# A two-layer convolution with weights made on the chip: loads ordered by marks, and a start-up rearranged

## The chip, the cores and the metric

One core of a Trainium2 chip runs the whole program. Its engines are TensorE (PE, with its weight loads PEld), VectorE (DVE), ScalarE (ACT), GpSimd (POOL) and SyncE (SP), which here issues DMA transfers and computes nothing. The metric is the time of one execution in microseconds.

## The reference

Two layers of the same form, each x = x + conv(groupnorm(x)), on x of shape (32, 32, 64, 256): 32 samples s, 32 positions b, 64 channels, length 256. The convolution has three taps, and its weights differ for every b and every l; they are made by a small network from z:

```python
h = jax.nn.relu(_ln(z @ W1 + b1, g1, be1))              # (32, 256, 128)
w = (h @ W2 + b2).reshape(B, L, CI, CO, K)              # 12288 weights for each (b, l)
hb = jax.nn.relu(_ln(z @ Wb1 + bb1, gb1, beb1))
bias = (hb @ Wb2 + bb2).transpose(0, 2, 1)
x_uf = jnp.stack([xp[..., i:i + L] for i in range(K)], axis=-1)
out = jnp.einsum('sbilk,bliok->sbol', x_uf, w) + bias[None]
```

`groupnorm` cuts the last axis into 32 groups of 8 and takes the mean and variance over all positions, channels and the 8 of the group, separately for each sample.

## The kernel before

**Units and steps.** A unit u is four positions (NT) by a quarter of the length (64 values, LT); a layer has UL = 32 units, the program U = 64. Each unit is worked in two halves of the output channels, so that there are 128 steps v = 2u + h. The main loop (L821) runs v from 1 to 127. In step v TensorE makes the weights of v in twelve groups (`weights`, L739) and, behind the first group's `make`, the convolution of step v - 1 (`products`, L665). `order` (L737) lists the groups: for each of four sets of eight channels the kinds 0, 2, 1. `make` (L615) fills a PSUM tile `pg` (three buffers); `take` (L626) evicts it with b2 added into the tile `wall`: VectorE takes kinds 0 and 1 and half of kind 2 (L634), ScalarE the other half of kind 2 in eight instructions (L645). `products` runs 288 matmuls in four bursts, each into one of two PSUM buffers `pc`, and VectorE adds each burst to the residual in `ring` (L685) and in layer 0 takes statistics of the result for the next layer's norm (`last_stats`, L341).

**Order by hand.** The whole program is emitted in a fixed order, and each engine executes its part in that order. `agenda(v)` (L781) lists what is emitted behind each of the twelve groups. Behind group 0 stands `after(v - 1)` (L725), all on SyncE: the store of the finished half, the load of four pieces of x for the statistics of the first norm (`load_pieces`, until step 42), the residual and the bias of step v + 1 (`load_residual`, `load_bias` with four transfers) and every fourth step the hidden layer (`load_hidden`). Behind group 2 stands `next_half` (L694): GpSimd normalizes half a unit from `raw` or `land` into `xn` (two instructions, L608), and SyncE loads the half after it: one transfer in layer 0, four in layer 1, whose rows are 128 bytes long (L177). Behind group 5 GpSimd adds the bias (`add_bias`, L566). The edges of a half are collected by ScalarE behind group 1 (`take_edges`, L581) and in every second step of layer 0 transposed by TensorE behind group 3 (`turn_edges`, L586), for the neighbours in layer 1.

**Start-up.** `first_phase` (L440) streams x in 22 units of four pieces through three slots of `ring` and one in `land`, while the small network runs in eight batches (`Batch`): ScalarE writes the hidden layer (L302) and the bias (L327), and issues their stores `hd` (L311) and `bd` (L333) itself. The first 18 units (`needed`) give the statistics that the first norm needs. Then come `Merge`, the tables `tab`, `starting` (L759: VectorE normalizes unit 0 in eight pieces, two halves by four cuts), the statistics of the last units, and step 1. The twelve groups of step 0 run inside this phase (`first_weights`).

Of the kernel before, what the change touches and what calls it, by code (L numbers as in the profile page):

```python
# [30 lines left out]
P = 128  # L31
# [12 lines left out]
def conv_layers(  # L44
# [39 lines left out]
    xe = [dram.tile([P, P], FP, name=f"xe_{u}") for u in range(UL)]  # L84
    hd = [dram.tile([P, 2 * BLK], FP, name=f"hd_{i}") for i in range(U // 4)]
    bd = [dram.tile([NT, 2, C, LT], FP, name=f"bd_{i}") for i in range(U // 2)]

# [75 lines left out]
    def load_half(u, k, buf=None):  # L163

        buf = raw if buf is None else buf
        n, q, bg = place_of(u)
        if n == 0:
            nc.sync.dma_start(out=by_slot(buf), in_=xp[u][:, k * NT // 2 : (k + 1) * NT // 2])
            return
        if k == 0:  # L170
            load_edges(u)
        for a in range(2):
            for h in range(NH):
                rows = slice((1 - a) * C + h * CH, (1 - a) * C + (h + 1) * CH)
                src = x1[u - UL][h][k * NT // 2 * S : (k + 1) * NT // 2 * S]
                src = src.rearrange("(t s) (o a m) -> a o t s m", s=S, a=2, m=MT)[a]
                nc.sync.dma_start(out=by_sample(buf)[rows, :, :, a : a + MT], in_=src)  # L177

# [43 lines left out]
    class Batch:  # L222
# [69 lines left out]
        def hidden(self, net):  # L292
            vec = self.w.vec
            ps = []
            for k in range(2):
                p = ps_g.tile([P, 2, BLK], FP, tag="pg", name="ph")
                ps.append(p)
                for r in range(2):
                    x = slice((2 * k + r) * R, (2 * k + r) * R + A + 1)
                    nc.tensor.matmul(p[:, r], self.w.wc[x, net], self.zq[x, net], start=True, stop=True)  # L300
            for k in range(2):
                nc.scalar.activation(  # L302
                    self.ht[net][k],
                    ps[k].rearrange("p r f -> p (r f)"),
                    AF.Relu,
                    bias=vec[:, 2 * net + 1 : 2 * net + 2],
                    scale=vec[:, 2 * net : 2 * net + 1],
                )
                if net:
                    continue  # L310
                nc.scalar.dma_start(out=hd[self.j * NR // 2 + k], in_=self.ht[0][k])  # L311

        def bias(self, i):
            n = 2 * M
            p = ps_c.tile([P, n], FP, tag="pc", name="pb")
            for b in range(2):
# [15 lines left out]
            )  # L332
            nc.scalar.dma_start(  # L333
                out=bd[i].rearrange("t b o l -> (b o) t l"), in_=bs.rearrange("p t a m -> p t (a m)")
# [105 lines left out]
    def first_phase(first_weights, first_bias, add_bias, starting):  # L440
# [22 lines left out]
        with tc.tile_pool(name="stage", bufs=1) as stage:  # L463
# [35 lines left out]

            for i in range(units):  # L500
                j, odd = divmod(i, 2)
# [32 lines left out]
                if i == 6:  # L534
                    for x in range(2):
                        load_hidden(x)
                if i == needed - 2:
                    load_half(0, 1, land)
                    load_residual(0)
                if i == needed - 1:  # L540
                    load_half(0, 0)
                    load_w2(0, CH, C)
                if i == needed:
                    first_bias()
                if i == needed + 1:
                    table.lay(table.spread(), [nc.vector.tensor_copy, nc.scalar.copy])
                    starting()
                first_weights(i - (needed - 11))
            load_residual(1)

    with tc.manual_schedule():
# [73 lines left out]

        def take(pg, n, kind, o0):  # L626

# [36 lines left out]

        def products(v):  # L665
            u, h = divmod(v, NH)
# [3 lines left out]
            for q in range(NB):  # L670
# [23 lines left out]
        def next_half(u, k):  # L694
# [29 lines left out]

        def after(v):  # L725

            u, h = divmod(v, NH)
            store(v)
            load_pieces(v + 1)
            if v + 2 < NH * U:  # L730
                load_residual(v + 2)
                load_bias(v + 2)
            if h == 1 and u % 2 == 1 and u + 3 < U:
                load_hidden((u + 3) // 2)

        starts = range(0, CH, OG)
        order = [(kind, o) for o in starts for kind in (0, 2, 1)]  # L737

        def weights(v, k, between=None):  # L739
# [5 lines left out]
            if between:  # L745
                between()
            take(pg, n, kind, o0)
            if kind == 1 and u % UL == UL - 1 and n + 1 < NL:
# [10 lines left out]
        def starting():  # L759
# [3 lines left out]
            cuts = [0] + [1 + e * (q + 1) for q in range(NB)]  # L763
            for j0, j1 in zip(cuts, cuts[1:]):
                for k in range(2):
                    normalize(0, k, bufs[k], nc.vector, j0, j1)
            load_half(1, 0)

        def first_bias():
            x = xn.rearrange("p n t j s -> p (n t j s)")  # L770
            h = x.shape[1] // 2
            load_bias(0, x[:, h : h + CH * LT].rearrange("p (o l) -> p o l", l=LT))

        first_phase(first_weights, first_bias, add_bias, starting)
# [52 lines left out]
        products(NH * U - 1)  # L827
        after(NH * U - 1)


# [92 lines left out]
```

## Time and profile before

| | us |
|---|---|
| three runs | 4000.01, 4010.09, 4016.39 |
| median | 4010.09 |
| the profiled execution, its own time | 4010.21 |
| its span (first to last instruction) | 4008.4 |
| TensorE busy in the span | 3810.9 |
| VectorE, GpSimd, ScalarE busy | 2592.2, 1939.5, 1285.8 |

The profile is one execution. A row of instructions gives start, duration, engine, line, operation, what it writes and reads, and in brackets the idle time of the engine before it and what ended it. "issue" as the one that ended it means that the engine waited for nothing that the profile shows. SPq and ACTq rows are the issue of transfers, not the transfers.

### The profile page before, as it was taken

Reading aid. Unit: us, or ns where it says so; the run is one execution under the profiler, and the core shown is the slowest. Engines: PE = TensorE matmul, PEld = TensorE weight load, DVE = VectorE, ACT = ScalarE, POOL = GpSimd, SP = SyncE. Lnnn points to the kernel's source line nnn. Section 1 sums busy time; section 2 is a strip of 40 time slices with the busy share of each in tenths; the row PEclk is TensorE's granted clock in tenths of the full one; section 3 lists DMA queues with packets and bytes.
Section 4 is the critical chain, followed back from the end, with each engine's and each line's share of the span. In section 5 each row is a group of like instructions: output and inputs, shape, how many; then the busy total and the mean of one; then the engine's idle time right before and its main releaser. Section 6 shows DMA issues by size and latency. Waiting matters only on the chain.

```text
span 4008.4 us, 185362 instructions
## 1 busy us (share of the span) xinstructions
PE 3810.9 (95%) x86548; PEld 3675.3 (92%) x86548; DVE 2592.2 (65%) x2954; ACT 1285.8 (32%) x4431; POOL 1939.5 (48%) x655
## 2 busy tenths in 40 slices
PE   6699999999999999999999999999999999999999
PEld 3499999999999999999989999999999999999998
DVE  4677777777777776666665555555555555555655
ACT  3423333323333333333323323323233233333332
POOL 2154445444544445544545545555546545645551
PEclk7799999999999999999999999999999999999999
DMA  8666556556556555445488878878788788788782
GB/s 271 233 201 195 180 177 193 177 172 195 177 178 196 173 168 159 134 153 156 134 196 154 148 132 160 145 147 151 140 166 141 140 156 141 147 150 140 157 146 87
DMA packets 644660, 657.76 MB, mean 164 GB/s; under 512 B 562600, under 2 KB 570160, under 8 KB 578096
## 3 DMA queue, kind: packets, MB, share of 16 engines
q1 hardware_dynamic: 624688, 633.30, 65.5%
q8 instruction: 677, 11.09, 1.2%
q10 hardware_dynamic: 19200, 12.59, 1.0%
q14 instruction: 95, 0.78, 0.1%
HBM read 496.91 MB, written 148.90 MB: 161 GB/s over the span
## 4 chain that ended last, share of the span: by engine, by line
PE 80%; DVE 6%; ACT 6%; issue 2%; DMA 1%; POOL 0%; SPq 0%; ACTq 0%; POOLq 0%; DVEq 0%
PE pg L622 49%; PE pc L676 24%; PE pg L623 6%; ACT wall L645 5%; DVE wall L634 4%; DMA bt<-bd 1%; DVE ring L685 1%; DVE parts L341 0%; POOL ring L566 0%; DVE xn L608 0%; PE pe L586 0%; DVE first_parts L723 0%; ACT rim L581 0%; PE over L371 0%; SPq L559 0%
## 5 line engine op out<-in xcount | busy, mean ns | idle before, releaser
L622 PE MATMUL pg<-hT,w2t 128*64 128x128 f32 x24576 | 2752.5, 274 | 26.7 <-issue 24.0
L623 PE MATMUL pg<-hT,w2t 128*64 128x128 f32 x24576 | 2753.3, 274 | 17.0 <-issue 16.7
L622 PEld LDWEIGHTS pg<-hT,w2t 128*64 128x64 f32 x24576 | 2689.0, 137 | 63.9 <-issue 37.9
L623 PEld LDWEIGHTS pg<-hT,w2t 128*64 128x64 f32 x24576 | 2689.2, 137 | 23.1 <-issue 22.7
L634 DVE TENSOR_TENSOR wall<-pg,b 128x1024 f32<-128x1024 f32 (+1 forms) x1536 | 1874.1, 1220 | 726.0 <-PE pg L623 720.1
L645 ACT ACTIVATE wall<-pg,b 64x128 f32<-64x128 f32 x4096 | 1158.8, 465 | 2596.1 <-DVE wall L634 2596.0
L566 POOL TENSOR_TENSOR ring<-ring,bt 128x2048 f32<-128x2048 f32 x127 | 578.1, 4552 | 1200.9 <-DMA bt<-bd 755.1
L676 PEld LDWEIGHTS pc<-wall,xn 128*32 128x32 f32 x36864 | 914.8, 110 | 110.3 <-issue 61.2
L676 PE MATMUL pc<-wall,xn 128*32 128x128 f32 (+1 forms) x36864 | 951.6, 262 | 64.1 <-issue 34.7
L685 DVE TENSOR_TENSOR ring<-pc,ring 128x512 f32<-128x512 f32 x512 | 353.9, 691 | 622.2 <-PE pc L676 617.9
L608 POOL TENSOR_TENSOR xn<-raw,tab 128x2112 f32<-128x2112 f32 x86 | 440.1, 5118 | 447.2 <-PE pc L676 433.7
L608 POOL TENSOR_TENSOR xn<-xn,tab 128x2112 f32<-128x2112 f32 x126 | 591.4, 4693 | 9.9
L608 POOL TENSOR_TENSOR xn<-land,tab 128x2112 f32<-128x2112 f32 x40 | 224.3, 5609 | 111.9 <-DMA land<-x 102.0
L341 DVE BATCH_NORM_STATS2 parts<-ring 128x6 f32<-128x256 f32 x512 | 192.1, 417 | 6.5
L723 DVE BATCH_NORM_STATS2 first_parts<-land 128x6 f32<-128x512 f32 x168 | 114.5, 681 | 0.6 <-DMA land<-in_xg_dram 0.6
L433 POOL COPY tab<-spot 64x1024 f32<-64x1024 f32 x28 | 29.0, 1035 | 94.1 <-ACT spot L420 93.2
L276 POOL TENSOR_TENSOR raw<-w2t,xn 128x256 f32<-128x256 f32 x16 | 10.3, 644 | 113.7 <-DVE xn L271 113.7
L300 PE MATMUL ph<-xn,wc 17*128 17x512 f32 x128 | 34.7, 771 | 26.7 <-DVE xn L266 15.3
L458 DVE BATCH_NORM_STATS2 first_parts<-ring 128x6 f32<-128x512 f32 x72 | 44.2, 676 | 17.3 <-DMA ring<-in_xg_dram 17.3
L300 PEld LDWEIGHTS ph<-xn,wc 17*128 17x128 f32 x128 | 10.0, 214 | 44.2 <-DVE xn L266 19.5
L302 ACT ACTIVATE xn<-ph,vec 128x1024 f32<-128x1024 f32 x32 | 37.5, 1198 | 9.8 <-ACT xn L302 5.7
L586 PEld LDWEIGHTS pe<-ident,rim 128*128 128x128 f32 x32 | 4.5, 139 | 36.0 <-ACT rim L581 36.0
(87 smaller groups left out, 368.8 us busy)
## 6 DMA issues: line engine op xcount, KB each, us to landing
bt<-bd SPq DMA_DIRECT2D x508, 256.0 KB, 10.6
ring<-in_xs_dram SPq DMA_DIRECT2D x64, 1024.0 KB, 11.1
x<-ring SPq DMA_DIRECT2D x64, 1024.0 KB, 4.9
ring<-x SPq DMA_DIRECT2D x64, 1024.0 KB, 9.5
out_dram<-ring SPq DMA_DIRECT2D x64, 1024.0 KB, 4.8
raw<-in_xp_dram SPq DMA_DIRECT2D x55, 1056.0 KB, 14.6
land<-in_xg_dram SPq DMA_DIRECT2D x46, 1024.0 KB, 8.2
raw<-x SPq DMA_DIRECT2D x128, 256.0 KB, 7.7
```

The lines of the kernel that those rows point to most:

```text
L300: nc.tensor.matmul(p[:, r], self.w.wc[x, net], self.zq[x, net], start=True, stop=True)
L341: nc.vector.bn_stats(out, y.rearrange("p o (a m) -> p o a m", a=2)[:, :, :, g * e : (g + 1) * e])
L458: nc.vector.bn_stats(first_parts[:, g, bg], slots[order[i]][:, k])
L566: nc.gpsimd.tensor_tensor(y, y, bts.pop(v), ALU.add)
L608: eng.tensor_tensor(o, i, tab[:, x, None, j0:j1].to_broadcast(list(o.shape)), op)
L622: nc.tensor.matmul(pg[0:C, k, :], w[:, k0 * C : (k0 + 1) * C], h0, start=True, stop=True)
L623: nc.tensor.matmul(pg[C:P, k, :], w[:, k1 * C : (k1 + 1) * C], h1, start=True, stop=True)
L634: nc.vector.tensor_tensor(place(rows, a), pg[rows].rearrange("p o (t m) -> p t m o", t=NT), b2[n][rows, kind, None, None, o0 : o0 + OG].to ...
L645: nc.scalar.activation(place(rows, a)[:, :, :, k], pg[rows, k].rearrange("p (t m) -> p t m", t=NT), AF.Identity, bias=b2[n][rows, kind, o0 ...
L676: nc.tensor.matmul(pc[t * S : (t + 1) * S, n0 - q * EB : n1 - q * EB, :], xn[:, u % 2, t, p, :], wall[:, t, a : a + (n1 - n0) * CH], start ...
L685: nc.vector.tensor_tensor(part, pc.rearrange("p (m a) o -> p o a m", a=2), part, ALU.add)
L723: nc.vector.bn_stats(first_parts[:, g, bg], lands[i % LAND])
```

## The change

Four things are changed together.

1. *Marks.* A mark is a transfer on SyncE of 16 bytes of `wall`, written by the eviction of a named group, to a scratch tensor. SyncE works in order, so what stands behind the mark is issued after that eviction. In step v the residual of v + 1 stands behind the mark of group 2, the half behind group 5 in layer 0, bias and hidden layer behind group 6; in layer 1 the four parts of a half stand behind groups 1, 4, 7 and 9. `after` is gone; store and pieces stay behind group 0. `add_bias` moves from group 5 to 9.
2. *Stores of the small network.* `hd` and `bd` are issued by SyncE.
3. *Start-up.* The bias and the residual of step 0 are loaded earlier, the bias into a free part of `w2`, and added at unit 15 instead of 19. The phase ends two units earlier; the statistics of the last two units, and the normalization of unit 1, go to step 1. `starting` normalizes two of the four cuts at once and the other two behind the first two additions of `products(0)`. In step 0 VectorE alone evicts kind 2. The slots of the last six units change.
4. *Order.* The last set of a step has its kinds in the order 2, 0, 1, and `turn_edges` stands behind group 7 instead of 3.

```diff
-        n, q, bg = place_of(u)
-        if n == 0:
-            nc.sync.dma_start(out=by_slot(buf), in_=xp[u][:, k * NT // 2 : (k + 1) * NT // 2])
-            return
-        if k == 0:
-            load_edges(u)
-        for a in range(2):
-            for h in range(NH):
...
+        nc.sync.dma_start(out=by_slot(buf), in_=xp[u][:, k * NT // 2 : (k + 1) * NT // 2])
+
+    def parts_of_half(u, k, buf):
+
+        def part(a, h):
...
+        return [lambda a=a, h=h: part(a, h) for a in range(2) for h in range(NH)]
...
-                nc.scalar.dma_start(out=hd[self.j * NR // 2 + k], in_=self.ht[0][k])
+                nc.sync.dma_start(out=hd[self.j * NR // 2 + k], in_=self.ht[0][k])
...
-            nc.scalar.dma_start(
+            nc.sync.dma_start(
                 out=bd[i].rearrange("t b o l -> (b o) t l"), in_=bs.rearrange("p t a m -> p t (a m)")
...
-        order = [i % 4 for i in range(needed - 2)] + [0, 1, 2, 1, 2, 1]
+        order = [i % 4 for i in range(needed - 2)] + [1, 2, 1, 2, 1, 2]
...
-            for i in range(units):
+            for i in range(needed + 2):
...
-                    add_bias(0)
...
+                if i == needed // 2:
+                    first_bias(half_w2[:, 0 : CH * LT])
+                if i == needed - 6:
+                    load_residual(0)
+                if i == needed - 3:
+                    add_bias(0)
                 if i == needed - 2:
                     load_half(0, 1, land)
-                    load_residual(0)
...
-                if i == needed:
-                    first_bias()
                 if i == needed + 1:
                     table.lay(table.spread(), [nc.vector.tensor_copy, nc.scalar.copy])
-                    starting()
+                    starting(0)
+                    starting(1)
                 first_weights(i - (needed - 11))
-            load_residual(1)
+        rest = [lambda i=i, k=k: stats(i, range(k, k + 2)) for i in range(needed + 2, units) for k in (0, 2)]
+        return rest
...
-                add_scalar(slice(C, P), CH)
+                (add if alone else add_scalar)(slice(C, P), CH)
...
                 nc.vector.tensor_tensor(part, pc.rearrange("p (m a) o -> p o a m", a=2), part, ALU.add)
+                if between:
+                    between(q)
...
-            u, k = (u, 1) if k == 0 else (u + 1, 0)
-            if u < U:
-                load_half(u, k, place_half(u, k))
+            u, k = half_after(u, k)
+            if UL <= u < U and k == 0:
+                load_edges(u)
...
+        def mark(v, k):
+
+            kind, o = order[k]
+            a = (3 * CH, 0, 2 * CH)[kind] + o
+            nc.sync.dma_start(out=marks[v : v + 1, k], in_=wall[0:1, 0, a : a + 4])
...
-        order = [(kind, o) for o in starts for kind in (0, 2, 1)]
+        order = [(kind, o) for o in starts for kind in ((2, 0, 1) if o == starts[-1] else (0, 2, 1))]
...
+            def cut(q):
+                if q < NB:
+                    for k in range(2):
+                        normalize(0, k, bufs[k], nc.vector, cuts[q], cuts[q + 1])
...
-        normalize(1, 0)
-        load_half(1, 1)
-        add_bias(1)
+
+        def second():
+            load_half(1, 0)
+            normalize(1, 0)
+            load_half(1, 1)
+
+        def cut_next(q):
+            cut(q + 2)
...
-            todo[0].append(lambda: after(v - 1))
-            todo[2].append(lambda: next_half(*((u + 1, 1) if h == 0 else (u + 2, 0))))
+            if v == 1:
+                todo[0].append(second)
+            todo[0].append(lambda: store(v - 1))
+            todo[0].append(lambda: load_pieces(v))
+            half = (u + 1, 1) if h == 0 else (u + 2, 0)
+            todo[2].append(lambda: next_half(*half))
+            x, k = half_after(*half)
+            loads = {}
             if v + 1 < NH * U:
-                todo[5].append(lambda: add_bias(v + 1))
+                loads[4 if v == 1 else 2] = [lambda: load_residual(v + 1)]
+                loads[6] = [lambda: load_bias(v + 1), lambda: hidden_after(v - 1)]
+                todo[9].append(lambda: add_bias(v + 1))
+            if x < UL:
+                loads[5] = [lambda: load_half(x, k, place_half(x, k))]
+            elif x < U:
+                for i, part in zip((1, 4, 7, 9), parts_of_half(x, k, place_half(x, k))):
+                    loads.setdefault(i, []).append(part)
+            if v == 1:
+                for i, f in enumerate(rest):
+                    todo[1 + i].append(f)
+                todo[2].append(lambda: load_residual(1))
+                todo[2].append(lambda: add_bias(1))
+            for i, fs in loads.items():
+                todo[i].append(lambda i=i: mark(v, i))
+                todo[i] += fs
...
                 if h == 1:
-                    todo[3].append(lambda: turn_edges(u))
+                    todo[7].append(lambda: turn_edges(u))
...
-                weights(v, k, (lambda: products(v - 1)) if k == 0 else None)
+                weights(v, k, (lambda: products(v - 1, cut_next if v == 1 else None)) if k == 0 else None)
```

## Rows read from the trace of the kernel before

**Rows 1.** The page: busy time of each engine, its share of the span, instructions.
```profile
PE 3810.9 (95%) x86548; PEld 3675.3 (92%) x86548; DVE 2592.2 (65%) x2954; ACT 1285.8 (32%) x4431; POOL 1939.5 (48%) x655
```

**Rows 2.** Windows: stretch, us, busy PE, PEld, DVE, ACT, POOL, clock, DMA, GB/s.
```profile
0.00:200.00 200.00, 127.50 (x968) 84.01 (x968) 107.52 (x199) 81.94 (x146) 31.99 (x49) 0.75 0.76 252
```

**Rows 3.** Chain of waits: start, us, what; bursts of `products` in layer 0.
```profile
228.40 6.32 PE pc L676 x249
...
468.82 7.28 PE pc L676 x288
499.11 7.14 PE pc L676 x288
527.55 7.28 PE pc L676 x288
```

**Rows 4.** Waits of TensorE: line and releaser: us in total, times, longest us.
```profile
PE pc L676 <- issue: 34.7, 87, 3.1
PE pe L586 <- ACT rim L581: 28.3, 32, 1.0
PE pg L622 <- issue: 24.0, 27, 2.3
PE pg L623 <- issue: 16.7, 21, 2.3
...
PE pc L676 <- ACT wall L645: 12.1, 61, 1.9
```

**Rows 5.** Timeline, end of a step in layer 1: ScalarE, VectorE, TensorE.
```profile
3520.34 2.25 ACT L645 ACTIVATE wall<-pg,b 64x128 f32<-64x128 f32 x8 [2.97 <-DVE wall L634]
...
3520.77 1.22 DVE L634 TENSOR_TENSOR wall<-pg,b 128x1024 f32<-128x1024 f32 x1 [0.53 <-PE pg L623]
...
3522.64 0.63 PE L676 MATMUL pc<-wall,xn 128*32 128x64 f32 x17 [0.17 <-ACT wall L645]
```

**Rows 6.** Timeline of ScalarE and VectorE: after and at stores that ScalarE issues.
```profile
86.22 0.47 ACT L327 ACTIVATE xn<-pb,vec 128x256 f32<-128x256 f32 x1 [0.44 <-PE ph L300]
...
167.20 4.38 ACTq L333 DMA_DIRECT2D bd<-xn  x1
...
168.51 0.15 DVE L384 TENSOR_TENSOR apart<-over,moments 128x9 f32<-128x9 f32 x1
```

**Rows 7.** Timeline of VectorE and GpSimd: `starting` and the first additions.
```profile
178.91 0.76 DVE L608 TENSOR_TENSOR xn<-raw,tab 128x576 f32<-128x576 f32 x1
...
181.05 4.76 DVE L608 TENSOR_TENSOR xn<-land,tab 128x576 f32<-128x576 f32 x1
...
194.69 4.84 DVE L458 BATCH_NORM_STATS2 first_parts<-ring 128x6 f32<-128x512 f32 x8
...
207.23 0.69 DVE L685 TENSOR_TENSOR ring<-pc,ring 128x512 f32<-128x512 f32 x1 [1.87 <-PE pc L676]
...
180.18 5.01 POOL L566 TENSOR_TENSOR ring<-ring,xn 128x2048 f32<-128x2048 f32 x1 [40.78 <-ACT tab L435]
```

**Rows 8.** The page: a DMA queue: packets, MB, share of 16 engines.
```profile
q8 instruction: 677, 11.09, 1.2%
```

**Rows 9.** TensorE after two long issue waits; the window at the second's burst.
```profile
3549.85 0.32 PE L622 MATMUL pg<-hT,w2t 128*64 128x128 f32 x1 [2.30 <-issue]
...
2368.86 0.87 PE L676 MATMUL pc<-wall,xn 128*32 128x128 f32 x12 [3.09 <-issue]
...
2363.00:2366.00 3.00, 2.72 (x102) 2.48 (x102) 0.69 (x1) 0.00 (x0) 0.27 (x1) 1.00 1.63 95
```

**Rows 10.** Windows: products at the change of layers; a step of layer 1.
```profile
2090.00:2101.60 11.60, 7.32 (x282) 6.98 (x283) 4.33 (x9) 0.05 (x1) 0.00 (x0) 1.00 0.88 227
...
3494.20:3501.40 7.20, 7.20 (x290) 7.11 (x292) 2.07 (x3) 0.00 (x0) 7.12 (x3) 1.00 0.02 5
3516.00:3522.00 6.00, 6.00 (x116) 6.00 (x113) 4.42 (x4) 3.03 (x13) 4.79 (x2) 1.00 1.02 110
3502.00:3516.00 14.00, 14.00 (x262) 14.00 (x260) 10.27 (x10) 5.45 (x20) 6.03 (x3) 1.00 1.00 245
```

More of the change, by code (lines that the diff above doesn't have):

```diff
@@ L85, in conv_layers @@
     hd = [dram.tile([P, 2 * BLK], FP, name=f"hd_{i}") for i in range(U // 4)]
+    marks = dram.tile([U * NH, 16, 4], FP, name="marks")
     bd = [dram.tile([NT, 2, C, LT], FP, name=f"bd_{i}") for i in range(U // 2)]
@@ L165, in load_half @@
         buf = raw if buf is None else buf
-        n, q, bg = place_of(u)
-        if n == 0:
-            nc.sync.dma_start(out=by_slot(buf), in_=xp[u][:, k * NT // 2 : (k + 1) * NT // 2])
-            return
-        if k == 0:
-            load_edges(u)
-        for a in range(2):
-            for h in range(NH):
[L174 to L177, printed above, removed]
+        nc.sync.dma_start(out=by_slot(buf), in_=xp[u][:, k * NT // 2 : (k + 1) * NT // 2])
+    def parts_of_half(u, k, buf):
+        def part(a, h):
+            rows = slice((1 - a) * C + h * CH, (1 - a) * C + (h + 1) * CH)
+            src = x1[u - UL][h][k * NT // 2 * S : (k + 1) * NT // 2 * S]
+            src = src.rearrange("(t s) (o a m) -> a o t s m", s=S, a=2, m=MT)[a]
+            nc.sync.dma_start(out=by_sample(buf)[rows, :, :, a : a + MT], in_=src)
+        return [lambda a=a, h=h: part(a, h) for a in range(2) for h in range(NH)]
     def residual(v):
@@ L542, in first_phase @@
                     load_w2(0, CH, C)
-                if i == needed:
-                    first_bias()
                 if i == needed + 1:
                     table.lay(table.spread(), [nc.vector.tensor_copy, nc.scalar.copy])
-                    starting()
+                    starting(0)
+                    starting(1)
                 first_weights(i - (needed - 11))
-            load_residual(1)
+        rest = [lambda i=i, k=k: stats(i, range(k, k + 2)) for i in range(needed + 2, units) for k in (0, 2)]
+        assert len(rest) == 2 * (RING - 1)
+        return rest
     with tc.manual_schedule():
@@ L624, in make, with take @@
             return pg
-        def take(pg, n, kind, o0):
+        def take(pg, n, kind, o0, alone=False):
             def place(rows, a):
@@ L663, in last_stats, with products @@
                     bn_stats(parts[:, g, bg, h, :], residual(v), g)
-        def products(v):
+        def products(v, between=None):
             u, h = divmod(v, NH)
@@ L701, in next_half, with half_after @@
             normalize(u, k, place_half(u, k))
-            u, k = (u, 1) if k == 0 else (u + 1, 0)
-            if u < U:
-                load_half(u, k, place_half(u, k))
+            u, k = half_after(u, k)
+            if UL <= u < U and k == 0:
+                load_edges(u)
+        def half_after(u, k):
+            return (u, 1) if k == 0 else (u + 1, 0)
         pieces = [(j, bg, g) for j in range(1, NQ) for g in range(FIRST[j]) for bg in range(BG)]
@@ L723, in piece, with hidden_after @@
             nc.vector.bn_stats(first_parts[:, g, bg], lands[i % LAND])
-        def after(v):
-            u, h = divmod(v, NH)
[L728 to L732, printed above, removed]
+        def mark(v, k):
+            kind, o = order[k]
+            a = (3 * CH, 0, 2 * CH)[kind] + o
+            nc.sync.dma_start(out=marks[v : v + 1, k], in_=wall[0:1, 0, a : a + 4])
+        def hidden_after(v):
+            u, h = divmod(v, NH)
             if h == 1 and u % 2 == 1 and u + 3 < U:
@@ L746, in weights @@
                 between()
-            take(pg, n, kind, o0)
+            take(pg, n, kind, o0, v == 0)
             if kind == 1 and u % UL == UL - 1 and n + 1 < NL:
@@ L763, in starting, with first_bias @@
             cuts = [0] + [1 + e * (q + 1) for q in range(NB)]
[L764 to L774, printed above, removed]
+            def cut(q):
+                if q < NB:
+                    for k in range(2):
+                        normalize(0, k, bufs[k], nc.vector, cuts[q], cuts[q + 1])
+            return cut
+        def first_bias(buf):
+            load_bias(0, buf.rearrange("p (o l) -> p o l", l=LT))
+        cut = starting()
+        rest = first_phase(first_weights, first_bias, add_bias, cut)
         bp = ctx.enter_context(tc.tile_pool(name="bias", bufs=1))
         load_bias(1)
-        normalize(1, 0)
-        load_half(1, 1)
-        add_bias(1)
+        def second():
[4 more added lines that the diff above has]
+            cut(q + 2)
         def agenda(v):
@@ L827, in conv_layers @@
         products(NH * U - 1)
-        after(NH * U - 1)
+        store(NH * U - 1)
 def _parameters(inputs, n):
```

## The prediction

> **What bounds the kernel now.** The page comes first: TensorE is busy for 95% of the span, every other engine for at most 65% [rows 1]. So a microsecond counts where TensorE idles, and there are two regions. The table by windows shows the first: in the first 200 us TensorE is busy for 127.5, at a mean granted clock of 0.75 [rows 2]. After that the kernel is 127 like steps v, each with one `products` burst and twelve `make` groups; in the chain of waits a burst starts 28.44 us after the one before (499.11 to 527.55) where nothing interferes, and 30.29 us (468.82 to 499.11) where the step has the transposes of `turn_edges` [rows 3]. The waits by engine say what TensorE idles for [rows 4]: "issue", which means that no semaphore of the program ended the wait, 75.4 us in three rows; the transposes at L586 waiting for ScalarE's rim copy, 28.3 us; `products` waiting for ScalarE's last eviction, 12.1 us. The rest of that list is start-up.
>
> **The change part by part.** Durations are those of the profiled execution: 4010.2 us, of which 4008.4 are span. The median of the runs shown, 4010.09, is the same.
>
> *A. `turn_edges` from group 3 to group 7.* The rim copy stands behind ScalarE's eviction of group 1 and is ready 0.9 us after TensorE asks (28.3 by 32 [rows 4]). Four groups later, some 7 us, it has long been done. The transposes themselves stay. 32 waits go: -28 us. Bounds: nothing (if they are late there as well) and -28.3. What is late next in these steps is the next group's weights, which are there. The store of the edges starts 7 us later; it is read a layer later.
>
> *B. Last three groups in the order 2, 0, 1.* Kind 2 has two evictions, VectorE and then ScalarE. Now it is the group before the last: ScalarE's starts at 3520.34 and takes 2.25, so it ends 0.05 before `products` at 3522.64, which had waited 0.17 [rows 5]. VectorE's last starts at 3520.77 and takes 1.22: 3521.99, some 0.5 us before TensorE was through with `make` (3522.64 less 0.17). Moved one group (1.75 us) forward, ScalarE is no longer last, and VectorE's eviction is in time. The row credits it with 12.1 us; if each of 128 steps has a gap of 0.17, partly booked as issue, it is 22. I take -15, bounds 0 and -22.
>
> *C. Start-up.* Four things. (1) ScalarE issues the 48 stores of `hd` and `bd`; most leave 0.4 to 0.5 us idle before its next instruction, as 0.44 before 86.22. Going back from 167 us from each instruction to what released it, I find about ten of them on the way, the first just before 86.22; on SyncE they cost ScalarE nothing: 10 x 0.46 = 4.6 us. Bounds: nothing, and 48 x 0.46 = 22. One of them took 4.38 us (167.20) and held ScalarE's next instruction of `mean` until 171.6; without it VectorE's subtraction, 168.51 to 168.66, is last: -2.9 [rows 6]. (2) `add_bias(0)` runs on GpSimd from 180.18 to 185.19, and beside it one VectorE piece of `starting` takes 4.76 us where its like takes 0.76; it moves to where no such piece runs. (3) All eight pieces of `starting` and eight `bn_stats` (4.84) stand before the first addition: 178.91 to 199.53, and the last of the four ends at 207.92, 29.0 after the first piece [rows 7]. After: two cuts of 3.5 and 2.8, then an addition, 0.75 of statistics and a cut of 2.8, twice; the last two additions follow TensorE's bursts of some 2.7 us. I get 17.5 us from first piece to last addition: -11.5, the 4.0 of (2) among them. (4) The price is in step 1. The eight `bn_stats` go there: 4.84 us on VectorE, whose groups then take 2.4 instead of 1.75 us four times. And SyncE must issue `load_half(1, 0)`, wait, issue `load_half(1, 1)`, which waits until GpSimd has read the first from `raw` (4.67), and only then `store(0)` and `load_pieces(1)`. That is 23 us after the first piece; with a megabyte each of half and store ahead, the pieces land three times 4.3 us later (a megabyte at 245 GB/s [rows 10]). VectorE waits some 5.5 us for them. So from last addition to `products(1)` it takes 27.9 (six groups of 1.22, 0.75 of statistics and 4.84: 12.9; the wait of 5.5; six groups and three pieces: 9.4) instead of the 20.5 of now (207.92 to 228.40 [rows 3]): +7.4. Sum: -4.6 - 2.9 - 11.5 + 7.4 = -12 us, bounds -22 and -3.
>
> *D. The loads held by marks.* Now SyncE issues store, pieces or residual, bias and half in one go behind the products. Nothing waits for these loads on TensorE: what it has from them is the "issue" idle. The queue named instruction moves 677 packets, 11.09 MB [rows 8], and the longest such waits stand in stretches with saturated transfers: 2.30 us before 3549.85, behind the four parts, and 3.09 before 2368.86, in a burst of products [rows 9]. With marks a step's volume is the same. In layer 1 the DMA share is 1.00 from 3502 to 3516 and 0.02 during products [rows 10]; at the rates of these rows a megabyte is 4.3 us (245 GB/s), a part of 0.26 MB 2.4 us (110 GB/s), a step's three megabytes and four parts 22 us. After, I order them by the times of the evictions: store, part, residual, part, bias, part, part. They still touch, end to end, from 8.5 to about 31 us after the burst's start, as now. But the parts come singly, not as one stretch of 10 us. I take -10 of the 75.4; bounds -35 and +20.
>
> The Trainium skill weighs against this part: "DMA: Bandwidth & Descriptors", section "Queues, rings and completion order", has each DMA engine go round its queues packet by packet, so that a fetch waits for a packet and not for all that stands in the other queue. By that rule spacing gains nothing while the engines stay busy, and D would be 0. "Runtime: NRT & Kernel Launch", section "Instruction fetch mechanics", calls the refill of 16 KiB blocks mostly hidden; the trace agrees on the blocks (11.09 MB in 677) and not on the hiding (75.4 us).
>
> The marks themselves: 3 a step in layer 0, 6 in layer 1, some 570; each takes some 0.4 us of SyncE, as the stores took of ScalarE [rows 6], and SyncE has nothing else to do. Queued behind a mark are all later loads and the next store; who waits for these is GpSimd's `add_bias` (off the path, with a step to spare) and its `normalize`. The wait of an eviction for the mark's read of the step before has 28 us. Cost 0. Should SyncE fall behind by a whole step, it is the slow rival.
>
> *E. Change of layers.* W2's slices go through the same queue in steps 62 and 63. Now `products` there take 11.6 us, 7.3 of them busy, with the DMA share at 0.88 [rows 10]. The volume stays: 0, bounds -8 and +8.
>
> Sum: -28 - 15 - 12 - 10 = -65 us, so 4010.2 - 65 = 3945 us.
>
> **The rivals.** *R1, the marks do not do what they say*: the queue stays as full as before and the issue waits are those of now; D is 0 and A, B, C hold: 3955. For it: the share of 1.00. It is also the result of the rule of the Trainium skill's page "DMA: Bandwidth & Descriptors" cited under D. Against: parts come apart. *R2, the transfers reach into the products (slower)*: in layer 1 they fill nearly the step, and the last part is held until the tenth group. If it lands 2 us later than I think, the DMA works through the first microseconds of each burst, where TensorE uses up instructions fastest (582 in 7.2 us, against 522 in the 14 after [rows 10]). The step at 2363 shows it: in the three first microseconds of that burst the share is 1.63, where it is 0.02 in the burst from 3494 [rows 9, 10], and 3.09 us are lost. With 2.8 us in every one of the 62 steps from 66 on, +174; A to C pay 55: 4129; it turns slower once more than 20 steps have it, and in two thirds 4070. Against: the same bytes in the same 28.5 us. *R3, spacing cures most of the fetch waits*: D at its bound of -35, and ScalarE's freeing counts double: 3945 - 25 - 10 = 3910. For it: single megabytes leave gaps once the pieces end at step 42. *R4, only the order pays*: SyncE, waiting in order on stores and evictions in the first phase, gives the start-up's 12 us back, D is 0, B 12: 4010 - 40 = 3970.
>
> **How the numbers follow.** Forecast 0.45, R1 0.2, R4 0.13, R3 0.12, R2 0.10. The forecast's own range is 3925 to 3965. The range takes in R1, R3 and R4 with the bounds of C and E, and leaves out R2 and the far ends: 3900 to 3985. About 0.5% (20 us) is what can be told from no change. All but R2 are faster by more than that; of R2 a little falls within, and R4 with D at +20 too: faster 0.87, same 0.05, slower 0.08.
>
> **What would show it.** Right: L586 without a wait for the rim; `products` without one for ScalarE's eviction; steps of 28.3 us where nothing interferes; no 4.8 us piece at L608; `products(1)` at about 216 us instead of 228.4. D right: issue waits of TensorE near 65 us, with fewer beyond 2 us. R1: 75 again. R2: waits of 2 to 3 us at `products` in layer 1, and a DMA share well above zero in their first 3 us. R4: `products(1)` still near 228. The prediction is wrong if TensorE gets a new releaser worth over 20 us, bias or halves that land late among them.

## The result, and the profile after

The changed kernel took 3956.1 us (median of 4 runs, 3950.31 to 3958.95), the kernel before, beside it, 4013.24: ratio 0.9859 [0.983, 0.9889]. 3945 was predicted, with a range of 3900 to 3985. The total is about right, but the parts are not: the order edits gave more than forecast, and the marks cost time where they were to save some.

The profiled execution took 3950.3 us (span 3948.5), 59.9 less than the profiled one before. By stages, from the start of each burst of `products` in the two traces: up to `products(1)` 228.4 became 213.0 (-15.4); 60 steps of layer 0, 1797.9 became 1757.8 (-40.1); the four steps at the change of layers -0.8; layer 1, 1838.4 became 1833.5 (-4.9); the end +1.3.

The page first, against [rows 1, 8]: TensorE has 6 us less work, and as much is fetched on the instruction queue.

```profile
PE 3804.8 (96%) x86548; PEld 3670.0 (93%) x86548; DVE 2595.5 (66%) x2958; ACT 1275.9 (32%) x4399; POOL 1940.5 (49%) x655
...
q8 instruction: 676, 11.08, 1.3%
```

The window of the first 200 us (columns as in [rows 2]): 13.8 us more work of TensorE done by then, at a mean granted clock of 0.84 instead of 0.75.

```profile
0.00:200.00 200.00, 141.34 (x1368) 98.65 (x1368) 120.62 (x220) 75.83 (x131) 43.52 (x53) 0.84 0.83 276
```

The chain of waits, against [rows 3]: the undisturbed step is 28.26 us (1300.43 to 1328.69) instead of 28.44, and one with the transposes of the edges 29.78 (1004.75 to 1034.53) instead of 30.29.

```profile
213.08 3.08 PE pc L681 x118
...
1004.75 7.29 PE pc L681 x284
1034.53 7.14 PE pc L681 x288
...
1300.43 7.14 PE pc L681 x288
1328.69 7.18 PE pc L681 x285
```

TensorE's waits, against [rows 4] (line and releaser: us in total, times, longest). The rim's row is gone, and the row of the last eviction has shrunk to one wait of VectorE. "Issue" has not shrunk but moved: in `products` it has doubled, from 34.7 to 71.1 us; of the weights' row one wait of 8.2 us in the start-up is nearly all that is left.

```profile
PE pc L681 <- issue: 71.1, 127, 3.4
PE pg L627 <- issue: 9.3, 4, 8.2
...
PE pc L681 <- DVE wall L639: 1.4, 1, 1.4
...
PE pg L628 <- issue: 0.6, 2, 0.3
```

I sorted all waits of TensorE over 0.06 us from `products(1)` on by their place in the step (before to after): rim 28.3 to 0; at the start of `products` (ScalarE's eviction 12.5, issue 8.5, GpSimd 1.1) 22.1 to 1.4; issue among the weights 43.6 to 5.2; issue inside `products` 23.6 to 68.7. Busy time fell by 2.8, and 0.6 of waiting for ScalarE came up among the weights. Together this is the 44.5 that this stretch lost. Here and below a wait that ends within 8.6 us of the burst's start counts as inside `products`. A delayed burst runs past that: counted by the instruction that waits, the issue waits go from 41.3 to 1.7 among the weights and from 25.9 to 72.2 inside `products`, so the shift is still clearer.

### The profile page after: what moved, and what is told of

Read it like the earlier page. It is cut to its first block, busy times and chain, and to the rows that moved or that the text cites. A ratio compares the mean times of both kernels' runs of the same rounds, so it can differ in the third digit from the quotient of the medians.

```text
span 3948.5 us, 186560 instructions
## 1 busy us (share of the span) xinstructions
PE 3804.8 (96%) x86548; PEld 3670.0 (93%) x86548; DVE 2595.5 (66%) x2958; ACT 1275.9 (32%) x4399; POOL 1940.5 (49%) x655
## 4 chain that ended last, share of the span: by engine, by line
PE 94%; issue 2%; DMA 2%; DVE 1%; ACT 0%; POOL 0%; SPq 0%; POOLq 0%; ACTq 0%; DVEq 0%
PE pg L627 62%; PE pc L681 24%; PE pg L628 6%; DMA hd<-xn 0%; DVE wall L639 0%; DMA wc<-in_L_conv_wc_dram 0%; DMA land<-in_xg_dram 0%; PE spread L416 0%; DMA w2t<-in_L_conv_z_dram 0%; DMA hT<-hd 0%; PE over L371 0%; PE pb L318 0%; PE pe L591 0%; ACT xn L302 0%; PE ph L300 0%
## 5 line engine op out<-in xcount | busy, mean ns | idle before, releaser
L681 PE MATMUL pc<-wall,xn 128*32 128x128 f32 (+1 forms) x36864 | 976.6, 262 | 77.1 <-issue 71.1
L327 ACT ACTIVATE xn<-pb,vec 128x256 f32<-128x256 f32 x32 | 14.5, 473 | 28.5 <-PE pb L318 27.9
```

The costliest lines, as they stand in the source:

```text
L681: nc.tensor.matmul(pc[t * S : (t + 1) * S, n0 - q * EB : n1 - q * EB, :], xn[:, u % 2, t, p, :], wall[:, t, a : a + (n1 - n0) * CH], start ...
```

## The experiments

Waits for instructions ("issue") differ between executions of the same kernel: 75.7 us in the first profile of before and 60.2 in a second, 73.8 and 69.1 for after. So kernels run on one chip are compared where they can be; ratios are each to the kernel before on the same chip. e1 to e5, e7 and the repeats c_before and c_after ran on one chip, e8, e5b and e6 on a second, e9 on a third. All runs are in one table; the issue columns count from `products(1)` on.

| run | median us | ratio [95%] | products(1) at | issue in products / among weights | layer 0 / layer 1 |
|---|---|---|---|---|---|
| e1_order | 3930.94 | 0.9856 [0.9837, 0.9876] | 229.9 | 22.9 / 23.4 | 1754.1 / 1803.0 |
| e2_nomark | 3913.11 | 0.9815 [0.9791, 0.9839] | 211.6 | 47.6 / 2.2 | 1741.0 / 1813.5 |
| e3_act_stores | 3950.08 | 0.9902 [0.9883, 0.992] | 223.1 | 67.3 / 1.7 | 1753.2 / 1833.7 |
| e4_parts_first | 3954.93 | 0.9921 [0.9901, 0.9942] | 211.0 | 39.2 / 5.0 | 1751.2 / 1840.6 |
| c_before | 3989.85 | one run | 228.6 | 17.0 / 33.9 | 1799.6 / 1817.3 |
| c_after | 3941.48 | 0.9886 [0.987, 0.9902] | 212.0 | 62.9 / 6.2 | 1751.5 / 1833.9 |
| e5_early | 3898.03 | 0.9776 [0.9762, 0.979] | 209.6 | 22.4 / 18.2 | 1741.2 / 1802.4 |
| e7_free_marks | 3907.77 | 0.9801 [0.9787, 0.9816] | 210.1 | 45.1 / 7.6 | 1744.8 / 1813.8 |
| e8_edges | 3956.43 | 0.9921 [0.9907, 0.9934] | 229.0 | 22.7 / 28.9 | 1772.5 / 1817.6 |
| e5b_early | 3903.26 | 0.9793 [0.9779, 0.9807] | 212.4 | 20.8 / 23.1 | 1741.8 / 1806.6 |
| e6_start | 3938.86 | 0.9876 [0.9859, 0.9892] | 201.2 | 47.2 / 30.9 | 1784.5 / 1808.2 |
| e9_start2 | 3899.89 | 0.9783 [0.9767, 0.98] | 206.8 | 19.1 / 21.1 | 1745.1 / 1801.9 |

**The order alone (e1), the edges alone (e8).** The kernel before with `turn_edges` moved and the last set reordered, and with the first of these only:

```diff
-        order = [(kind, o) for o in starts for kind in (0, 2, 1)]
+        order = [(kind, o) for o in starts for kind in ((2, 0, 1) if o == starts[-1] else (0, 2, 1))]
...
-                    todo[3].append(lambda: turn_edges(u))
+                    todo[7].append(lambda: turn_edges(u))
```

> The kernel before with two edits alone: turn_edges behind group 7, and the last set in the order 2, 0, 1. My theory: these two are additive and are most of the gain in the steps: TensorE's 28.3 us of waiting for the rim and the gap of about 0.17 us at the start of each products (some 20 us) go, the issue waits stay at about 75 us where they are now (about 40 in the weights' groups): 48 us less than the kernel before, ratio 0.988. Rival (the stall goes elsewhere, the next fetch of instructions takes up the freed time): at most 30 us less.

> The kernel before with one edit of the change alone: the edges of the first layer are turned behind the eighth set of the additions instead of the fourth. Theory (the 29 us for which TensorE stands at the turning are all on the path): the rim waits go, nothing takes their place, 26 to 32 us less, ratio 0.992 to 0.9935; the gaps of some 21 us at the start of the products stay, and the order of the last set is worth the rest of the 57 us. Rival (part of the wait is only moved to the products behind it, and the order of the last set gives more): ratio 0.995 to 1.0.

The edges alone are worth 29.2 us (3985.67 - 3956.43), as expected; both together 53.8 (3984.78 - 3930.94, on another chip) where 48 were expected, so the order of the last set some 25. In e8's waits the rim is gone and the wait for ScalarE's eviction stands as before; in e1's it is gone too:

```profile
PE pc L676 <- issue: 30.7, 87, 2.6
PE pg L622 <- issue: 21.6, 25, 2.5
...
PE pc L676 <- ACT wall L645: 12.1, 59, 1.9
```

```profile
PE pc L676 <- issue: 22.6, 49, 2.6
...
PE pg L622 <- issue: 14.6, 25, 1.3
...
PE pg L623 <- issue: 9.2, 15, 2.2
```

Two edits of the order thus give by themselves the ratio of the whole change (0.9856 and 0.9859). The rest of the change is worth nothing as a sum: a gain and a loss in it cancel. On the chip of e1, where the change has 0.9886 (c_after), it costs some 12 us, at the edge of the intervals.

**The stores of the small network back on ScalarE (e3).** The change, with `nc.scalar` for SyncE at the two lines of `hd` and `bd`.

> The changed kernel with the stores hd and bd issued by ScalarE again. My theory: their issue on ScalarE lies on the way to the first norm, so the first normalized piece starts 8 to 14 us later than 161 us, and what SyncE loses by them (3.8 us of VectorE waiting for the last bd store) comes back: products(1) 4 to 10 us later than 213.0, and so the whole. Rival (the start-up gained by the order of the pieces and the moved bias alone): products(1) within 3 us of 213.0.

`products(1)` comes at 223.1 us, 10 to 11 later than in the two profiles of the change, where 4 to 10 were expected; the whole time is 8.6 us above c_after's, within the intervals. One store holds ScalarE for 11.18 us here, the last row of its queue:

```profile
156.19 0.37 ACTq L333 DMA_DIRECT2D bd<-xn  x1
...
157.11 11.18 ACTq L333 DMA_DIRECT2D bd<-xn  x1
```

So this edit is worth more than the 7.5 us of the forecast, though within the new start-up: in the kernel before, the same store held ScalarE for 4.38 us [rows 6].

**No marks (e2), marks that wait for nothing (e7).** e2 leaves out the line `todo[i].append(lambda i=i: mark(v, i))`; e7 keeps every mark, but it copies a constant:

```diff
-            nc.sync.dma_start(out=marks[v : v + 1, k], in_=wall[0:1, 0, a : a + 4])
+            nc.sync.dma_start(out=marks[v : v + 1, k], in_=ident[0:1, 0:4])
```

> The changed kernel without the marks; every load stands where it stood in SyncE's order, held by nothing but its own buffers. My theory: holding the loads moves TensorE's waits for instructions from the weights' groups into the products and takes none away; without marks the time is that of the changed kernel within 8 us (ratio to the kernel before 0.984 to 0.988), with issue waits of 65 to 85 us in the steps, of which at least 25 are back in the weights' groups and the products' share in layer 1 falls from 46 to under 30. Rival 1 (the marks gain by spreading the loads): 15 to 40 us slower than the changed kernel. Rival 2 (the marks lose by pushing transfers into the products): 15 to 30 us faster.

> The changed kernel with as many marks at the same places of SyncE's queue, but each copies 16 bytes of a constant tile instead of an evicted one, so that it waits for no eviction and holds nothing back. Theory (the holding costs: it brings the loads later and into the next step's products): the time falls to that of the kernel without marks, ratio 0.980 to 0.984, waits in the products of the second layer 25 to 35 us. Rival (the extra transfers and instructions themselves cost): ratio 0.984 to 0.989 as with the marks of the change, waits in those products 40 to 50 us.

Both are faster than the change, by 28 us (c_after 3941.48, e2 3913.11) and 34 (e7 3907.77), all on one chip. e2's theory, a time within 8 us and waits back among the weights, was wrong, and its second rival right; e7 came out as expected. The transfers of the marks cost nothing that shows; their holding does. TensorE's issue rows, first c_after, then e7:

```profile
PE pc L681 <- issue: 65.3, 120, 3.4
PE pg L627 <- issue: 9.1, 3, 8.5
```

```profile
PE pc L681 <- issue: 50.6, 84, 4.4
...
PE pg L627 <- issue: 8.1, 3, 7.5
```

Without holding, the waits do not return to the weights; they shrink in the products. Not all of the loss is waiting: from c_after to e2 TensorE's waits behind `products(1)` fall by 19 us and its busy time, for the same matmuls, by 11 (3649.8 to 3639.3). Why it is busy longer is not shown.

> The changed kernel once more, beside the others of this call. Theory (the marks cost about 17 us, the order of the edges and of the last set gives about 57 us): ratio to before 0.983 to 0.990, waits for instructions 60 to 80 us, of them 35 to 50 us inside the products of the second layer and under 3 us among its additions. Rival (what the first chip showed of the stalls was chance): the stalls lie elsewhere here.

> The kernel before once more, profiled on the chip of the three runs beside it, so that waits can be compared row by row without a change of chip. Theory: TensorE's waits in the steps for instructions (issue) add up to 45 to 80 us, two thirds of them among the additions of the second layer; the rim waits (about 28 us) and the gaps at the last set (12 to 22 us) are there as in the first profile. Rival: the waits for instructions on this chip are small (under 30 us), and then the 75.7 us of the first profile were a trait of that chip.

Both came out by the first halves of these texts, except that in c_before 33.9 of 60.2 us, a little over half and not two thirds, lie among the weights, and 18.6 of them in the second layer.

**Loads at the times of before (e5).** No marks, and in layer 1 the loads stand where the kernel before has them (e5b is the same kernel on another chip):

```diff
+            late = v < NH * UL
-                loads[4 if v == 1 else 2] = [lambda: load_residual(v + 1)]
-                loads[6] = [lambda: load_bias(v + 1), lambda: hidden_after(v - 1)]
+                loads[4 if v == 1 else 2 if late else 0] = [lambda: load_residual(v + 1)]
+                loads.setdefault(6 if late else 0, []).extend([lambda: load_bias(v + 1), ...])
...
-                for i, part in zip((1, 4, 7, 9), parts_of_half(x, k, place_half(x, k))):
-                    loads.setdefault(i, []).append(part)
+                loads.setdefault(5 if late else 2, []).extend(parts_of_half(x, k, place_half(x, k)))
```

> The changed kernel without marks; in the second layer the loads are issued where the kernel before issues them (store, residual, bias and hidden units at the first set, the four parts together behind the normalization at the third), in the first layer as in the run without marks. Theory (how late in a step the loads go out decides where TensorE runs out of instructions: late loads put the stalls into the products that follow): waits inside the products of the second layer fall from 31 to about 10 us, those among its additions rise from 1 to about 12 us, second layer about 1803 us as in the run with the order alone, ratio about 0.979. Rival (the start-up and the spread of the loads have no part, the stalls only wander): the sum of the waits in the second layer stays at 32 us, ratio 0.9815 as without marks.

> The kernel without marks and with the early loads in the second layer once more, as the one to compare the next with on the same chip. Theory: ratio 0.976 to 0.979 again, waits for instructions about 40 us. Rival (the earlier 0.9776 was the chip's): 0.980 or more.

The waits in layer 1's products fell from 31.3 (e2) to 11.0 us, those among its weights rose from 0.8 to 12.6, and layer 1 took 1802.4 us, as in e1 (so `add_bias`, which stands behind group 9 here and behind group 5 in e1, costs nothing there). This is the fastest kernel here, 1.1% below the change on the same chip (0.9776 and 0.9886); e5b's 0.9793, just above the 0.976 to 0.979 expected, agrees within the intervals.

Where the transfers lie shows in the first 3 us of a burst. Adding up all packets of SyncE's queue in the 60 steps from 66 on, the engines busy of 16 in the first, second and third microsecond are 8.7, 1.9, 0.1 in c_before; 23.8, 15.0, 4.4 in c_after (packets of one engine overlap in the records, hence over 16); 19.0, 9.7, 1.9 in e2; 10.9, 3.2, 0.4 in e5. One step as an example, the same in each, by windows (columns as in [rows 2]), first the change, then e5. TensorE works 2.06 of 3.00 us at a DMA share of 0.77, and all of 3.00 at 0.02:

```profile
3402.30:3405.30 3.00, 2.06 (x77) 1.78 (x77) 0.00 (x0) 0.00 (x0) 3.00 (x1) 1.00 0.77 61
```

```profile
3362.80:3365.80 3.00, 3.00 (x122) 2.96 (x124) 0.69 (x1) 0.00 (x0) 0.00 (x0) 1.00 0.02 5
```

**The four parts earlier, still marked (e4).**

```diff
-                for i, part in zip((1, 4, 7, 9), parts_of_half(x, k, place_half(x, k))):
+                for i, part in zip((1, 2, 4, 5), parts_of_half(x, k, place_half(x, k))):
```

and in layer 1 the residual behind group 6, bias and hidden layer behind group 8.

> The changed kernel with another assignment of marks in layer 1: the four parts of a half behind groups 1, 2, 4 and 5, the residual behind 6, bias and hidden layer behind 8. My theory: what delays instructions at the products is the parts with rows of 128 bytes, two of which now reach into them; with whole megabytes there instead, TensorE's issue waits at products in layer 1 fall from 46 to 10 to 25 us and those in the weights' groups rise by no more than 10: 10 to 30 us faster than the changed kernel. Rival (any transfer there delays a fetch as much): issue waits as in the changed kernel, time within 8 us.

The waits in layer 1's products fell (46.5 in c_after, 20.1 here), but a new one took their place: before `make`, twice in a step of layer 1, TensorE waits 0.2 us for ScalarE, 24.0 us in all. So the time did not fall, and the gain of 10 to 30 us that was expected did not come.

```profile
PE pc L681 <- issue: 41.9, 66, 4.6
PE pg L627 <- ACT wall L650: 24.0, 122, 1.5
...
PE pg L627 <- issue: 4.7, 2, 4.3
```

Why this wait appears when only SyncE's order changes was not tested.

**The start-up again (e6, e9).** e5 with two edits: of W2's second half (3 MB) only 8 channels are loaded early, the rest behind the first phase's last loads; and in step 1 SyncE issues pieces and store ahead of its wait for GpSimd. e6 issues the pieces ahead of the store in every step, e9 behind it as the change does.

```diff
-                    load_w2(0, CH, C)
+                    load_w2(0, CH, CH + OG)
...
                     starting(1)
+                    load_w2(0, CH + OG, C)
...
-            todo[0].append(lambda: store(v - 1))
             todo[0].append(lambda: load_pieces(v))
+            todo[0].append(lambda: store(v - 1))
```

> That kernel with the start-up changed in two places: of the second half of the first layer's W2 (3 MB in one transfer) only the first 8 channels are loaded before the last loads of the first phase, the other 24 behind the last of them; and in the first step SyncE issues the load of pieces and the store before it waits for GpSimd's normalization. Theory (W2's 3 MB and SyncE's place in the queue set the end of the start-up): VectorE's waits for a landing at the first pieces (0.8 to 3.8 us) and for the loaded pieces (3.4 to 5.7 us) go, TensorE's wait of some 8 us before the products goes, products(0) 4 to 8 us earlier, products(1) 5 to 10 us earlier, ratio 0.0015 to 0.0025 below the kernel beside it. Rival (the 16 DMA engines are full from 140 to 175 us, so an order of loads gives nothing, and the later channels are then late): products(1) within 2 us, ratio the same, with new waits of TensorE for W2.

> The run before with the changed start-up, and SyncE's queue put back at one place: the load of pieces is issued behind the store again, as in the change and in the kernel before (ahead of the store it went out in the first microseconds of each step of the first layer, into the products). Theory (1 MB moved into the products is what cost the stalls): the DMA engines busy in the second to fourth microsecond of a first-layer step fall from 8 to 10 of 16 to under 1, waits for instructions in these products from 37 to about 8 us, first layer 1784 to about 1742 us, products(1) 201 to 205 us, ratio 0.975 to 0.9775. Rival (W2's late slices or the different place of the code cost them): the waits stay over 25 us, ratio 0.985 to 0.989.

e6's start-up came out a little better than expected (`products(1)` 11.2 us earlier than in e5b), and still the kernel was 35.6 us slower. The swap lets the megabyte of pieces go out as the burst of `products` begins; behind the store, which needs the burst's last addition, it leaves some 8 us into the step. In the second to fourth microsecond of layer 0's steps 5.9, 10.7 and 10.7 engines are now busy (0.6, 0.3, 0.1 in e5b; means of 60 steps, a third of them without pieces), and layer 0's waits in `products` rise from 8.0 to 37.1 us, 29 of the 43 us that the layer is longer. With the two lines back in order (e9) they are 7.6 us and layer 0 takes 1745.1 instead of 1784.5. TensorE's largest issue row, first of e6, then of e9:

```profile
PE pc L682 <- issue: 50.9, 60, 4.1
```

```profile
PE pc L682 <- issue: 22.6, 42, 4.6
```

SyncE's queue and TensorE in the same step, first e6 (the pieces 0.2 us after the burst's start at 1011.19, a wait of 1.40 us later in the burst, a step of 31.33 us), then e9 (8.4 us after the start at 994.76, no such wait, 29.64 us):

```profile
1011.41 0.33 SPq L727 DMA_DIRECT2D land<-in_xg_dram  x1
...
1018.14 1.08 PE L682 MATMUL pc<-wall,xn 128*32 128x64 f32 x35 [1.40 <-issue]
...
1020.87 0.32 SPq L577 DMA_DIRECT2D x<-ring  x1
```

```profile
1002.76 0.32 SPq L577 DMA_DIRECT2D x<-ring  x1
1003.13 0.42 SPq L727 DMA_DIRECT2D land<-in_xg_dram  x1
```

e9 missed its ratio, 0.9783 [0.9767, 0.98] where 0.975 to 0.9775 was expected, and `products(1)`, 206.8 for 201 to 205, and cannot be told from e5. The last burst of `products(0)` now waits for instructions, while W2's late slices are loaded; that these cause the wait was not tested. Of the 11.2 us 2.8 to 5.6 are left.

```profile
181.98 0.32 PE L682 MATMUL pc<-wall,xn 128*32 128x64 f32 x8 [4.56 <-issue]
```

## Why the prediction was right, and where it was wrong

*A, the edges: right.* -28 forecast; the rim wait is 0 in the trace after (28.3 before), and e8 gives 29.2 us. The transposes themselves stand without a gap.

*B, the order of the last set: right in kind, too small.* -15 was taken from a row that credits 12.1 us and an upper bound of 22. The gaps at the start of `products` went from 22.1 to 1.4, and e1 less e8 gives some 25 (two chips): the upper bound was the truth, because the part of each gap booked as issue was the same wait. The end of a step of layer 1, against [rows 5]: ScalarE's last eviction now ends at 3521.49, VectorE's at 3522.64, and `products` start at 3523.04.

```profile
3519.22 2.27 ACT L650 ACTIVATE wall<-pg,b 64x128 f32<-64x128 f32 x8 [1.22 <-DVE wall L639]
...
3521.41 1.23 DVE L639 TENSOR_TENSOR wall<-pg,b 128x1024 f32<-128x1024 f32 x1 [0.52 <-PE pg L628]
...
3523.04 1.19 PE L681 MATMUL pc<-wall,xn 128*32 128x64 f32 x40
```

*C, the start-up: -15.4 against -12, close by luck, as errors cancel.* The first piece moved from 178.91 to 161.08, by 17.8 us instead of 7.5; with the stores back on ScalarE (e3) it comes at 175.61, so they are worth 14.5 of it. From it to the last addition it took 22.4 us instead of the predicted 17.5 (161.08 to 183.45), as VectorE stood 3.83 us for the landing of the last store of the bias. From there to `products(1)` it took 29.6 instead of 27.9 (whose terms add up to 27.8), with the wait for the pieces almost as predicted, 5.70 for 5.5. The piece of 4.76 us [rows 7] takes 0.76 now, from `land` as from `raw`. VectorE's timeline:

```profile
161.08 0.76 DVE L613 TENSOR_TENSOR xn<-raw,tab 128x576 f32<-128x576 f32 x1
...
167.02 0.76 DVE L613 TENSOR_TENSOR xn<-land,tab 128x576 f32<-128x576 f32 x1 [3.83 <-DMA bd<-xn]
...
169.96 0.69 DVE L613 TENSOR_TENSOR xn<-land,tab 128x512 f32<-128x512 f32 x1
...
182.76 0.69 DVE L690 TENSOR_TENSOR ring<-pc,ring 128x512 f32<-128x512 f32 x1 [0.85 <-PE pc L681]
...
201.32 0.69 DVE L733 BATCH_NORM_STATS2 first_parts<-land 128x6 f32<-128x512 f32 x1 [5.70 <-DMA land<-in_xg_dram]
```

What I left out was SyncE's own queue: the store that VectorE waits for stood behind a load that took SyncE 7.75 us to issue, with W2's 3 MB ahead of it. In e9, with W2 split and the pieces issued ahead of the wait for GpSimd, neither VectorE's 3.83 us nor its 5.70 for the pieces is left; which edit removed which was not separated.

```profile
152.63 7.75 SPq L451 DMA_DIRECT2D ring<-in_xg_dram  x1
```

*D, the marks: wrong in sign, and the step that failed* is "They still touch, end to end, from 8.5 to about 31 us after the burst's start, as now." The bytes were the same, but all loads except the first part left later, the last part 27.3 instead of 24.7 us after its burst's start. The last packet of SyncE's queue ended 32.5 instead of 30.7 us after that start, 2.8 instead of 1.2 us into the next burst, and 1.4 us in e5 (medians of 58 steps of layer 1). -10 was forecast with +20 as the upper bound. Against the loads of the kernel before, as D was meant, the first two traces leave +5 to +9 (44.5 less A's 28.3 and B's 21 to 25), and e1 and c_after, on one chip, +26 behind `products(1)`: layer 1 takes 1833.9 instead of 1803.0 us. Against the same kernel without marks (e2) it is 18 us by ratio (0.9859 less 0.9815, two chips) and 28 on one chip. The idea of spacing was half right: among the weights the issue waits did go, from 43.6 to 5.2. But in `products` they rose from 23.6 to 68.7, where TensorE uses up its instructions fastest [rows 10]. So rival R2 is what happens, at 0.55 us a step of layer 1 (12.4 to 46.5 us over 62 steps) instead of its 2.8, and in exchange for the waits among the weights. "Against: the same bytes in the same 28.5 us" was no argument: the phase of the step decides, not the volume, as e6 and e9 show with one load in two places.

That TensorE's issue waits are late instructions is inferred from their place: in six steps of layer 1 of the trace after (104 to 109), each starts to run again 1.1 to 1.7 us before the next packet of the instruction queue starts, and of all 132 over 0.15 us from `products(1)` on in that trace 128 end 1.0 to 1.7 us before one. A packet is also slower itself beside other transfers: in the trace before its median is 1.0 us where SyncE's queue keeps under 5% of the engines busy, and 1.5 where its records add up to over 100%. How much of the waits, of up to 3.4 us, that makes and how much is queueing was not separated. One burst shows the pattern, a wait behind 46 and behind 128 matmuls:

```profile
3402.32 1.41 PE L681 MATMUL pc<-wall,xn 128*32 128x64 f32 x46
3404.66 3.27 PE L681 MATMUL pc<-wall,xn 128*32 128x128 f32 x128 [0.94 <-issue]
3408.40 2.83 PE L681 MATMUL pc<-wall,xn 128*32 128x128 f32 x104 [0.47 <-issue]
```

The Trainium skill's rule ("DMA: Bandwidth & Descriptors", section "Queues, rings and completion order": an engine goes round its queues packet by packet) made D 0 if the engines stay busy either way. The runs differ from what I drew from it: 1 MB moved by some 8 us changed the waits of layer 0 by 29 us. The engines were not equally busy in the place that counts, so this does not speak against the rule itself.

*E, the change of layers:* 0 forecast, -0.8 measured.

That the total came within 11 us of the forecast is luck in part: B and C gave 9 to 13 us more than forecast and D 15 to 19 less.

*The rivals.* R1 (the marks do nothing) fails by e2 and e7. Its time, 3955, is the nearest to the 3956.1 measured, by luck. R4 (only the order pays) has the right net result and 3970, by other causes: the start-up did gain its 15 us, and the marks took it back in part (first pair) or more (the chip of e1). R3 had the cure of the fetch waits without its price.

## What to carry to other kernels

Where an engine runs unrolled code and the profile shows issue waits, list for each load not only its size but the stretch of the step in which it moves: keep the stretches with the most instructions per microsecond free, and let loads go early enough that the last one lands before them. A hold on a load should be priced by where the transfer ends, not by the spacing that it gives. Price the waits of a group by the gap at its place in every step, not by the row that names one releaser: the part booked as issue went with it.

## What the runs showed of the hardware

A transfer of SyncE or ScalarE held its issuing engine for long while large ones were under way: 7.75 us for a load issued 5.8 us after W2's 3 MB, and 11.18 us for a store of 128 KB on ScalarE in e3, issued 4.5 us after them on SyncE; most issues of one transfer before took 0.33 to 0.55 us. What holds the engine was not tested. Waits for instructions cost 40 to 78 us in the steps of all these kernels, 1 to 2% of the time; the Trainium skill calls the refill "mostly hidden" ("Runtime: NRT & Kernel Launch", section "Instruction fetch mechanics"). The traces agree as far as 98% of the time goes, but show a price that grows with the transfers beside it: in the same 60 steps of layer 0, 7.6 us in e9 and 37.1 in e6. The sum in one kernel differed by up to 15.5 us between two profiled executions, on two chips (75.7 and 60.2 for the kernel before).
